# Transposing m through DRAM in every second set of a batched matrix square root

## The chip, the cores and the metric

The kernel runs on one core of a Trainium2 chip. The metric is device time in microseconds (us), and the time of a kernel is the median of its runs. Five engines work side by side, each through its own queue in order: TensorE (PE, with its weight loads shown as PEld), VectorE (DVE), ScalarE (ACT), GpSimd (POOL) and SyncE (SP), which here only issues DMAs.

## The reference

The input `x` has 32 batches of 32 channels of 128x128 matrices in f32. Two layers follow each other, each with a residual. Layer 0 normalises `x` over groups of two channels and then takes the square root of each of the 1024 matrices by five coupled Newton-Schulz steps:

```
Y = A / |A|;  Z = I
for _ in range(5):
    T = 0.5 * (3 I - Z @ Y)
    Y = Y @ T
    Z = T @ Z
x = x + Y * sqrt(|A|)
```

Layer 1 normalises again, takes a 2D Fourier transform, multiplies a few low modes by weights that mix channels, transforms back and adds to `x`. The change concerns layer 0 alone.

## The kernel before

**Tiles and sets.** A set is four channels of one batch, held as a tile of 128 partitions by 4x128 f32 (256 KB). There are 256 sets, 8 to a batch. The five Newton-Schulz steps are rewritten as matrix polynomials: a quartic in m, then an updated m, then a second quartic in the new m, and a last half step. TensorE computes `lhsT.T @ rhs`, so every product needs its left factor transposed. The kernel therefore carries m and a scaled transpose mb of it.

**One set, step by step** (`newton`, L400, and `quartic`, L364). `products` (L304) issues four 128x128 matmuls into one of eight PSUM banks; each f32 matmul is two PE instructions in the trace. `transposed` (L310) issues four PE transposes, one instruction each (L313). `taken` (L271, its operation on L276) copies a bank out on ACT with a factor. `plus` (L279, L282) copies it out on DVE with a factor and an addend. `plus_eye` (L290) makes r = mb + identity on POOL (L294 and L301).

The first quartic makes v from mb and m, needs v transposed plus r (that is w), and gives q from v and w. Then y is made from q and m, the new m from q and y. The new m is transposed on PE (`transposed(m)`), copied out as mb, and the second quartic follows with m and mb. Then come w (tile t) and y4 from q with m and y, then t from w and q, and the last product t with y is added to the input tile xt (L420).

**Far sets.** Sets of batches 1 to 18 (`is_far`, 144 sets) do not transpose v on PE. DVE transposes the 32x32 blocks of v into a tile named turn (L373), SP writes it to a DRAM tile called held (L375), SP reads it back with the blocks in their transposed places into w (one DMA on L386 for the first quartic, four DMAs of 32 partitions each on L383 for the second), and POOL adds r (L388). The first quartic reads v with a stride of four elements (`wide` is False), the second reads it in runs of 32 (`wide` is True). All other sets transpose v on PE.

**What sets the order.** The order is traced by hand: nine lanes hold one set each, the outer loop counts rounds, and in each round every lane advances its set's generator by one `yield`. `yield from rest` (rest is a pair) is two rounds. A far set has 13 such rests. A new far set may start three rounds after the last, if a lane is free. The tile framework then orders each engine's instructions by a plan of readiness, except those wrapped in `kept`, which stay in traced order: all DMA issues and the normalisation (L341, L348) among them. So SP's queue is exactly in traced order.

**Buffers.** `rooms` gives for each tile name two counts of buffers, the second from a pool that is open until 158 sets have ended (`MORE`). `four` (L263) goes round them.

**Beside it.** The same loop interleaves `prep` (statistics of the next batch), `settle` (store of xt to DRAM on L428, folds on POOL), `forward` and `spectrum` of layer 1. The later part of the kernel multiplies modes and transforms back; the change does not touch it.

Of the kernel before, what the change touches and what calls it, by code (L numbers as in the profile page):

```python
# [29 lines left out]
F32 = mybir.dt.float32  # L30
AF = mybir.ActivationFunctionType
ALU = mybir.AluOpType
# [4 lines left out]
P = 128  # L37
# [8 lines left out]
QA = 3 + 12 ** (1 / 3)  # L46
QR = 2 * QA - 9
QD = 39 / QA
EYE = 36 / 16
QS = EYE / QD  # L50
MS = -QA * QS
# [17 lines left out]
def conv_preact_kernel(  # L69
# [8 lines left out]
    nc = tc.nc  # L78

    const = ctx.enter_context(tc.tile_pool(name="const", bufs=1))  # L80
    dram = ctx.enter_context(tc.tile_pool(name="dram", bufs=1, space=DRAM))
# [5 lines left out]
    eye1 = const.tile([P, 1, P], F32, name="eye")  # L87
    nc.vector.tensor_scalar_mul(eye1[:, 0, :], ident, EYE)
    eye = eye1.to_broadcast([P, 4, P])
# [57 lines left out]
    def bank():  # L147
        return ps8.tile([P, 4, P], F32, tag="ps", name="ps")
# [36 lines left out]
    kept = tc.keep_in_program_order  # L185

    def prep(b, made):
# [12 lines left out]
        for i in range(C // 4):  # L200
# [37 lines left out]
        nc.vector.tensor_scalar_mul(  # L238
            nn, n.rearrange("p g c -> p (g c)"), P * (1.5 / EYE) ** 2
        )  # L240
# [17 lines left out]

    rooms = dict(b=(4, 2), xt=(10, 4), x=(3, 2), r=(5, 2), v=(3, 3), w=(3, 2), q=(4, 2), y=(4, 2))
    rooms.update(m=(4, 2), mb=(2, 1), t=(3, 2), y4=(2, 2), turn=(0, 4))  # L260
    turns = dict.fromkeys(rooms, 0)

    def four(tag, more):  # L263
        n, m = rooms[tag]
        if more:
            turns[tag] += 1
            if turns[tag] % (n + m) >= n:
                return early.tile([P, 4, P], F32, tag=tag + "_early", name=tag, bufs=m)
        return sets.tile([P, 4, P], F32, tag=tag, name=tag, bufs=n)

    def taken(ps, tag, more, f=1.0):  # L271
        t = four(tag, more)
        if f == 1.0:
            nc.scalar.copy(t, ps)
        else:
            nc.scalar.mul(t, ps, f)  # L276
        return t

    def plus(ps, f, t, tag, more):  # L279

        s = four(tag, more)
        nc.vector.scalar_tensor_tensor(s, ps, f, t, ALU.mult, ALU.add)  # L282
        return s

    def blocks(t):


        return t.rearrange("p c x -> p (c x)").rearrange("p (a c j) -> p a c j", a=4, c=4)

    def plus_eye(mb, far, more):  # L290

        r = four("r", more)
        if far:
            nc.gpsimd.tensor_tensor(  # L294
                blocks(r).rearrange("p a c j -> p c a j"),
                mb.rearrange("p c (a j) -> p c a j", a=4),
                eye.rearrange("p c (a j) -> p c a j", a=4),
                ALU.add,
            )
        else:  # L300
            nc.gpsimd.tensor_tensor(r, mb, eye, ALU.add)  # L301
        return r

    def products(lhsT, rhs):  # L304
        ps = bank()
        for j in range(4):
            nc.tensor.matmul(ps[:, j, :], lhsT[:, j], rhs[:, j], start=True, stop=True)  # L307
        return ps

    def transposed(t):  # L310
        ps = bank()
        for j in range(4):
            nc.tensor.transpose(ps[:, j, :], t[:, j, :], ident)  # L313
        return ps

    def is_far(b):
        return 0 < b < FIRST
# [43 lines left out]
        ready.append((xt, m, mb, plus_eye(mb, is_far(b), has_more(b, g))))  # L361
        yield

    def quartic(m, mb, r, far, more, wide):  # L364


        v = plus(products(mb, m), -1 / (QA * QR * QS), m, "v", more)
        if far:


            t = four("turn", more)
            form = "p c (b i) -> p b c i" if wide else "p c (i b) -> p b c i"
            nc.vector.transpose(blocks(t), v.rearrange(form, b=4))  # L373
            held = dram.tile([P, 512], F32, name="turn", tag="turn", bufs=8)
            kept(nc.sync.dma_start(out=held, in_=t.rearrange("p c x -> p (c x)")))  # L375
            yield from rest
            w = four("w", more)
            wb = blocks(w).rearrange("p a c j -> p a (c j)")
            if wide:
                for b in range(4):  # L380
                    rows = slice(32 * b, 32 * b + 32)
                    src = held[:, P * b : P * b + P].rearrange("(a i) x -> i a x", a=4)
                    kept(nc.sync.dma_start(out=wb[rows], in_=src))  # L383
            else:
                src = held.rearrange("(a i) (b x) -> (i b) a x", a=4, b=4)
                kept(nc.sync.dma_start(out=wb, in_=src))  # L386
            yield from rest
            nc.gpsimd.tensor_tensor(w, w, r, ALU.add)  # L388
            w = blocks(w).rearrange("p a c j -> p c a j")
        else:  # L390
            yield from rest
            w = plus(transposed(v), 1.0, r, "w", more)
        yield from rest
        q = plus(products(v, w), 1 / (16 * QS * QS), eye, "q", more)
        yield from rest
        return q

    rest = (None, None)

    def newton(g, sn, xt, m, mb, r, far, more):  # L400


        q = yield from quartic(m, mb, r, far, more, False)
        y = taken(products(q, m), "y", more, 1 / MS)
        yield from rest
        m = taken(products(q, y), "m", more, MS)
        yield from rest
        mb = taken(transposed(m), "mb", more, QR * QS / MS)
        r = plus_eye(mb, far, more)
        yield from rest  # L410
        q = yield from quartic(m, mb, r, far, more, True)
        pw, py = products(q, m), products(q, y)
        w, y = taken(pw, "t", more, 1 / MS), four("y4", more)
        for j in range(4):
            c = 4 * g + j
            nc.scalar.mul(y[:, j, :], py[:, j, :], sn[:, c : c + 1])  # L416
        yield from rest
        t = plus(products(w, q), -0.5 * EYE / 1.5, eye, "t", more)
        yield from rest
        nc.vector.tensor_tensor(xt, products(t, y), xt, ALU.add)  # L420
        yield
# [575 lines left out]
    while todo or any(lanes) or posts or specs or prods or backs:  # L997
# [3 lines left out]
        for i in range(LANES):  # L1001
            step(norms)
            step(loads)
            far = todo and is_far(todo[0][0])
            under_way = [is_far(lane[0]) for lane in lanes if lane]
            room = far or under_way.count(False) + 0.6 * under_way.count(True) < LESS
            if lanes[i] is None and todo and room and rounds >= due:
                due = max(due, rounds - 1) + (FAR if far else NEAR)
                while norms:
                    step(norms)  # L1010
                b, g = todo.pop(0)
                xt = ready[0][0]
                lanes[i] = (b, g, xt, newton(g, made[b][3], *ready.pop(0), far, has_more(b, g)))
                if stages:
                    stage()
                if not todo:
                    loads.append(weights())
            if lanes[i] is not None:
                b, g, xt, steps = lanes[i]
# [80 lines left out]
```

## Time and profile before

| what | value |
|---|---|
| median of 3 runs | 3109.61 us (3102.69 to 3109.81) |
| the profiled execution, its own time | 3100.66 us |
| span of that execution, first to last instruction | 3098.6 us |
| mean granted TensorE clock | 0.983 |
| PE busy, PEld busy | 2948.7 us, 2828.6 us |
| DVE, POOL, ACT busy | 2340.0, 1998.0, 1704.0 us |
| DMA | 636.78 MB, mean 206 GB/s |

A busy time is the union of an engine's instructions in the trace. The span can be cut into stretches of time: the far sets fill about 105 to 1610 us, the other sets and layer 1 the rest. Matmuls are pipelined, so their listed durations (about 277 ns each) overlap, and what one costs is read from the distance of starts. For SP the trace shows only issue times of DMAs; a wait of another engine for a DMA tells when it landed.

### The profile page before, as it was taken

How to read it: one execution, taken by the hardware profiler on the slowest of the kernel's cores; microseconds unless marked ns; L12 is line 12 of the kernel's file. 1: busy time of each engine (PE TensorE's matmuls, PEld its weight loads, DVE VectorE, ACT ScalarE, POOL GpSimd, SP SyncE). 2: the span in 40 equal slices, each digit the busy share in tenths (PEclk: the TensorE clock that was granted, in tenths of full speed). 3: DMA queues.
4: the chain of work that ended last, by engine and by line, in shares of the span. 5: the costliest groups of instructions: out<-in, count | busy, mean ns of one | idle time of the engine just before them, and what ended most of it. 6: DMA issues, size and time to landing. Idle time of an engine off the chain costs nothing. (4 is left out here: it accounts for less than half of the span.)

```text
span 3098.6 us, 79471 instructions
## 1 busy us (share of the span) xinstructions
PE 2948.7 (95%) x29760; PEld 2828.6 (91%) x29760; DVE 2340.0 (76%) x5178; ACT 1704.0 (55%) x4153; POOL 1998.0 (64%) x2312
## 2 busy tenths in 40 slices
PE   6999999999999999999999999999999998999994
PEld 6899999999999999999999998998899988899983
DVE  6788887888888787788877555788778766878654
ACT  3566556666665665666654444555454544555552
POOL 3567677677776666677665434768677764777453
PEclk9999999999999999999999999999999999999996
DMA  4576676666666666676743466667676876766666
GB/s 130 164 216 207 202 217 211 210 213 214 212 209 208 209 207 183 201 212 208 219 146 100 143 217 214 226 228 235 206 250 209 269 233 211 236 208 204 194 218 221
DMA packets 475150, 636.78 MB, mean 206 GB/s; under 512 B 97040, under 2 KB 255248, under 8 KB 474768
## 3 DMA queue, kind: packets, MB, share of 16 engines
q1 hardware_dynamic: 361872, 425.88, 42.8%
q10 hardware_dynamic: 112896, 205.83, 21.7%
q8 instruction: 237, 3.88, 0.5%
q14 instruction: 145, 1.19, 0.1%
HBM read 402.42 MB, written 229.11 MB: 204 GB/s over the span
## 5 line engine op out<-in xcount | busy, mean ns | idle before, releaser
L388 POOL TENSOR_TENSOR w<-w,r 128x512 f32<-128x512 f32 x288 | 366.3, 1276 | 324.3 <-DMA w<-turn 274.8
L307 PE MATMUL ps<-w,v 128*128 128x128 f32 x4096 | 554.6, 279 | 18.0 <-DVE w L282 7.7
L341 ACT ACTIVATE b<-b,a_off,a_scr 128x128 f32<-128x128 f32 x1024 | 468.7, 490 | 154.6 <-issue 48.1
L307 PE MATMUL ps<-y,q 128*128 128x128 f32 x4096 | 527.0, 277 | 6.2 <-ACT d L893 2.1
L307 PEld LDWEIGHTS ps<-w,v 128*128 128x128 f32 x4096 | 504.0, 194 | 25.1 <-POOL w L388 11.0
L307 PEld LDWEIGHTS ps<-y,q 128*128 128x128 f32 x4096 | 490.5, 193 | 9.6 <-issue 2.6
L433 POOL TENSOR_TENSOR fold<-xt 128x256 f32<-128x256 f32 x512 | 363.8, 731 | 204.5 <-DVE xt L420 192.2
L282 DVE SCALAR_TENSOR_TENSOR q<-ps,eye 128x512 f32<-128x512 f32 x512 | 348.0, 680 | 156.8 <-PE ps L307 151.5
L827 POOL TENSOR_TENSOR yt<-yt,d 128x512 f32<-128x512 f32 x248 | 311.2, 1282 | 153.7 <-ACT d L893 116.0
L301 POOL TENSOR_TENSOR r<-mb,eye 128x512 f32<-128x512 f32 x112 | 142.7, 1274 | 311.3 <-ACT mb L276 298.8
L348 POOL TENSOR_SCALAR x<-xt,a_nm,a_sc 128x128 f32<-128x128 f32 x736 | 322.7, 451 | 19.5 <-DVE a_n L231 19.5
L416 ACT ACTIVATE y<-ps,a_t_s 128x128 f32<-128x128 f32 x1024 | 291.4, 367 | 58.1 <-PE ps L307 57.6
L202 DVE BATCH_NORM_STATS2 a_st<-xs 128x6 f32<-128x128 f32 x1024 | 229.2, 278 | 108.7 <-DMA xs<-in_xt 107.9
L307 PE MATMUL ps<-m,q 128*128 128x128 f32 x2048 | 276.4, 278 | 8.1 <-DVE q L282 5.2
L307 PE MATMUL ps<-x,b 128*128 128x128 f32 x2048 | 277.0, 279 | 6.8 <-POOL x L348 5.6
L307 PE MATMUL ps<-m,mb 128*128 128x128 f32 x2048 | 276.7, 279 | 6.6 <-ACT d L893 4.3
L307 PE MATMUL ps<-x,q 128*128 128x128 f32 x2048 | 277.8, 279 | 3.3 <-DVE q L282 1.6
L307 PE MATMUL ps<-y,t 128*128 128x128 f32 x2048 | 275.1, 277 | 2.1 <-DVE t L282 2.0
L276 ACT ACTIVATE t<-ps 128x512 f32<-128x512 f32 x256 | 152.3, 595 | 223.1 <-PE ps L307 214.4
L307 PE MATMUL ps<-q,t 128*128 128x128 f32 x2048 | 274.9, 278 | 0.0
L373 DVE STREAM_TRANSPOSE turn<-v 128x512 f32<-128x512 f32 x288 | 262.0, 910 | 4.6
L307 PEld LDWEIGHTS ps<-m,q 128*128 128x128 f32 x2048 | 251.6, 193 | 10.7 <-DVE q L282 5.8
(148 smaller groups left out, 5768.2 us busy)
## 6 DMA issues: line engine op xcount, KB each, us to landing
turn<-turn SPq DMA_DIRECT2D x288, 256.0 KB
b<-in_x ACTq DMA_DIRECT2D x256, 256.0 KB
xt<-in_xt ACTq DMA_DIRECT2D x256, 256.0 KB
xs<-in_xt ACTq DMA_DIRECT2D x256, 256.0 KB
mid<-xt SPq DMA_DIRECT2D x256, 256.0 KB
yt<-mid SPq DMA_DIRECT2D x128, 512.0 KB
out<-yt SPq DMA_DIRECT2D x120, 512.0 KB
w<-turn SPq DMA_DIRECT2D x144, 256.0 KB
```

Of the source, the lines that this page charges most:

```text
L202: nc.vector.bn_stats(st[:, 4 * i + c, :], tiles[i][:, c, :])
L276: nc.scalar.mul(t, ps, f)
L282: nc.vector.scalar_tensor_tensor(s, ps, f, t, ALU.mult, ALU.add)
L301: nc.gpsimd.tensor_tensor(r, mb, eye, ALU.add)
L307: nc.tensor.matmul(ps[:, j, :], lhsT[:, j], rhs[:, j], start=True, stop=True)
L341: nc.scalar.activation(t, x, AF.Identity, bias=offset[:, c], scale=scale[:, c])
L348: nc.gpsimd.tensor_scalar(m[:, j, :], xt[:, j, :], nm[:, c // 2 : c // 2 + 1], sc[:, c : c + 1], ALU.add, ALU.mult,)
L373: nc.vector.transpose(blocks(t), v.rearrange(form, b=4))
L388: nc.gpsimd.tensor_tensor(w, w, r, ALU.add)
L416: nc.scalar.mul(y[:, j, :], py[:, j, :], sn[:, c : c + 1])
L433: nc.gpsimd.tensor_tensor(f[:, :, 64 * half : 64 * half + 64], xt[:, :, 0:64], xt[:, :, 64:128], op)
L827: engine.tensor_tensor(yh, yh, d, op)
```

## The change

`quartic` takes its two factors, the scale and the addend by argument, and its transposition through DRAM becomes a generator of its own, `turned`, which always reads v in runs of 32 and always reads back by four DMAs. `newton` uses it for the first and second quartic of all far sets. In far sets of even number (`g % TURNED == 0`, 72 of 144) `turned` also transposes m, in place of the four PE transposes. The result mt is taken as the right factor of the second quartic and its addend, so that this quartic gives the transposed polynomial, and the products behind it are in another order: w from q and mt, t from q and w, then q and t scaled (tile y4), then the last product with y. mb is taken directly from the product that gives m and serves r only. A DVE operation whose addend is mt is issued as four of 128x128, since mt lies in another layout. Such a set has 14 rests. Buffer counts change in `rooms`.

```diff
+TURNED = 2
...
+    rooms.update(mt=(0, 3), turn=(0, 4), b=(4, 1), m=(4, 2), y=(4, 4), r=(5, 3), v=(3, 4), w=(3, 2))
...
-    def quartic(m, mb, r, far, more, wide):
-        v = plus(products(mb, m), -1 / (QA * QR * QS), m, "v", more)
+    def turned(v, tag, more):
+        t = four("turn", more)
+        nc.vector.transpose(blocks(t), v.rearrange("p c (b i) -> p b c i", b=4))
+        held = dram.tile([P, 512], F32, name="turn", tag="turn", bufs=12)
+        kept(nc.sync.dma_start(out=held, in_=t.rearrange("p c x -> p (c x)")))
+        yield from rest
+        w = four(tag, more)
+        wb = blocks(w).rearrange("p a c j -> p a (c j)")
+        for b in range(4):
+            rows = slice(32 * b, 32 * b + 32)
+            src = held[:, P * b : P * b + P].rearrange("(a i) x -> i a x", a=4)
+            kept(nc.sync.dma_start(out=wb[rows], in_=src))
+        yield from rest
+        return w
+
+    def quartic(left, right, f, add, r, far, more):
+        ps = products(left, right)
+        v = four("v", more)
+        whole = len(add.shape) == 3
+        for c in [slice(0, 4)] if whole else range(4):
+            nc.vector.scalar_tensor_tensor(
+                v[:, c] if whole else v[:, c].rearrange("p (a j) -> p a j", a=4),
+                ps[:, c] if whole else ps[:, c].rearrange("p (a j) -> p a j", a=4), f, add[:, c], ALU.mult, ALU.add
+            )
         if far:
...
+            w = yield from turned(v, "w", more)
             nc.gpsimd.tensor_tensor(w, w, r, ALU.add)
...
-        m = taken(products(q, y), "m", more, MS)
-        yield from rest
-        mb = taken(transposed(m), "mb", more, QR * QS / MS)
-        r = plus_eye(mb, far, more)
...
+        pm = products(q, y)
+        m = taken(pm, "m", more, MS)
+        if far and g % TURNED == 0:
+            r = plus_eye(taken(pm, "mb", more, QR * QS), far, more)
+            mt = yield from turned(m, "mt", more)
+            mt = blocks(mt).rearrange("p a c j -> p c a j")
+            q = yield from quartic(m, mt, 1 / (QA * QA * QS), mt, r, far, more)
+            w = taken(products(q, mt), "t", more, 1 / MS)
+            yield from rest
+            t = plus(products(q, w), -0.5 * EYE / 1.5, eye, "t", more)
+            yield from rest
+            t = scaled(products(q, t), g, sn, "y4", more)
+        else:
...
         yield from rest
         nc.vector.tensor_tensor(xt, products(t, y), xt, ALU.add)
```

The `else` branch is the code of before. The DRAM tile held goes from 8 buffers to 12.

More of the change, by code (lines that the diff above doesn't have):

```diff
@@ L362, in staged @@
         yield
-    def quartic(m, mb, r, far, more, wide):
-        v = plus(products(mb, m), -1 / (QA * QR * QS), m, "v", more)
-        if far:
[L371 to L375, printed above, removed]
-            yield from rest
[L377 to L387, printed above, removed]
+    def turned(v, tag, more):
[21 more added lines that the diff above has]
+            )
+        if far:
+            w = yield from turned(v, "w", more)
             nc.gpsimd.tensor_tensor(w, w, r, ALU.add)
@@ L398, in conv_preact_kernel, with scaled @@
     rest = (None, None)
+    def scaled(ps, g, sn, tag, more):
+        y = four(tag, more)
+        for j in range(4):
+            c = 4 * g + j
+            nc.scalar.mul(y[:, j, :], ps[:, j, :], sn[:, c : c + 1])
+        return y
     def newton(g, sn, xt, m, mb, r, far, more):
-        q = yield from quartic(m, mb, r, far, more, False)
+        fm = -1 / (QA * QR * QS)
+        q = yield from quartic(mb, m, fm, m, r, far, more)
         y = taken(products(q, m), "y", more, 1 / MS)
         yield from rest
-        m = taken(products(q, y), "m", more, MS)
-        yield from rest
-        mb = taken(transposed(m), "mb", more, QR * QS / MS)
-        r = plus_eye(mb, far, more)
[L410 to L418, printed above, removed]
+        pm = products(q, y)
[11 more added lines that the diff above has]
+        else:
+            yield from rest
+            mb = taken(transposed(m), "mb", more, QR * QS / MS)
+            r = plus_eye(mb, far, more)
+            yield from rest
+            q = yield from quartic(mb, m, fm, m, r, far, more)
+            pw, py = products(q, m), products(q, y)
+            w = taken(pw, "t", more, 1 / MS)
+            y = scaled(py, g, sn, "y4", more)
+            yield from rest
+            t = plus(products(w, q), -0.5 * EYE / 1.5, eye, "t", more)
         yield from rest
```

## The prediction

> **What bounds the kernel now.** I read the page first, then the busy times of the two halves of the span, then PE's waits in the far stretch, then the timeline. Of the page, the busy shares:
>
> ```profile
> PE 2948.7 (95%) x29760; PEld 2828.6 (91%) x29760; DVE 2340.0 (76%) x5178; ACT 1704.0 (55%) x4153; POOL 1998.0 (64%) x2312
> ```
>
> The stretch in which far sets run, and the rest (columns: length; PE, PEld, DVE, ACT, POOL busy; granted clock; DMA share; GB/s):
>
> ```profile
> 105.00:1610.00 1505.00, 1484.98 (x13345) 1442.30 (x13347) 1230.00 (x2782) 909.42 (x2247) 1051.31 (x1166) 0.99 0.67 206
> 1610.00:3098.00 1488.00, 1385.12 (x15788) 1310.51 (x15788) 1041.70 (x2196) 752.61 (x1807) 902.41 (x1078) 0.97 0.65 210
> ```
>
> In the far stretch PE is busy 98.7% and its weight loads 95.8%; DVE has 18% idle, POOL 30%, ACT 40%, and the DMA engines a third. 144 sets in 1505 us are 10.45 us a set. All that PE waits for there, by the waits of PE in that window, is about 20 us:
>
> ```profile
> PE ps L307 <- POOL w L388: 7.5, 6, 3.8
> PE ps L313 <- ACT sw L472: 4.9, 4, 3.7
> PE ps L307 <- DVE xt L420: 1.9, 1, 1.9
> ```
>
> So PE's instruction rate bounds this stretch. What an instruction costs is read from starts on the timeline, not from its listed duration:
>
> ```profile
> 805.91 1.06 PE L307 MATMUL ps<-q,t 128*128 128x128 f32 x8
> 806.80 0.60 PE L313 MATMUL ps<-ident,m 128*128 128x128 f32 x4
> 807.24 1.06 PE L307 MATMUL ps<-w,v 128*128 128x128 f32 x8
> ```
>
> Eight instructions (four products) start 0.89 us apart, 0.111 us each; the four transposes of m take 807.24 - 806.80 = 0.44 us, 0.110 us each, though the page lists 277 ns for one.
>
> **What the Trainium skill says.** "Perfetto Trace Analysis", section "Identifying the Most-Contended Engine", warns that matmul busy time tells little of headroom and gives the weight-load share instead. Here both stand over 95% in the far stretch, so they agree. "TensorE: Matmul & The Clock Gate", "Part 4: PE-mode transpose", gives about 275 ns for a PE transpose in a kernel; the trace has 273 to 277 ns as duration, but 110 ns as spacing, and the spacing is the price. "VectorE: DVE Perf Modes", "The three transpose paths", says that DVE transposes only 32x32 blocks, which is why blocks have to change places through DRAM. "DMA: Bandwidth & Descriptors", "Latency and other measured facts", puts most of a DMA's fixed cost of about 2 us down to the receipt from memory, more at high load. In the far stretch the shortest time from the end of a DVE transpose to the issue of its read-back, which waits for the write to land, is 2.1 us: it agrees.
>
> **The change, part by part.**
>
> *Removed from PE.* 72 sets lose 4 transposes: 288 x 0.110 us = 31.7 us. The number of products stays at ten a set (before q m, q y, w q, t y behind the second quartic; after q mt, q w, q t, t y). A right factor in the blocked layout costs nothing new: w is one, and its products keep the 0.89 us spacing. Since PE is full, all 31.7 us lie on the path, unless PE waits more.
>
> *DVE.* A transpose has two prices on the timeline, 0.70 us in runs and 1.12 us with stride:
>
> ```profile
> 805.43 0.70 DVE L373 STREAM_TRANSPOSE turn<-v 128x512 f32<-128x512 f32 x1
> 810.05 1.12 DVE L373 STREAM_TRANSPOSE turn<-v 128x512 f32<-128x512 f32 x1
> ```
>
> All become short: 144 x 0.42 = 60 us less. New are 72 x 0.70 = 50 us. The addition of mt in four pieces has no row; 128x128 on DVE costs 0.21 us without PSUM (the eye row of the groups), a quarter of the whole operation 0.17. I bound four at 0.68 (nothing extra) to 1.12 us and take 0.90: 72 x 0.22 = 16 us. Net +6 us on 1230 of some 1475, 84% instead of 82%. It costs nothing while DVE's idle time covers it. The new transpose waits for ACT's m in the same step (0.60 us, timeline), and other sets' v, q and t stand behind it on DVE. That is under 1 us x 72, within DVE's 275 us of idle time; PE uses those results two rounds later. If that cover failed, PE would lose what the rest below prices.
>
> *ACT and POOL.* The same copies, mb now straight from the product and two rests earlier, with r on POOL; r lives longer and has eight buffers for it. Additions on L388 are as many as before. Nothing is added. Moved past: mb's copy and r now stand before the turn's DVE and SP work in the same step; both engines have room (62% and 71% of the shorter stretch).
>
> *SP.* Per set today: two writes of 0.33, one single read 0.38, four part reads 2.1 on average (1.97 to 2.88 in the timeline), the store on L428 0.56: 3.7 us of 10.45, 35%. After, per pair of sets: 5 writes 1.65, 20 part reads 10.5, 2 stores 1.1: 13.3 us of 20.5, 65%. SP is in traced order, so every read stands behind some other set's write, which waits for a DVE transpose.
>
> *DMA.* ACT's loads, 294 of 256 KB, fill 25.8% of 1000 us (DMA view, 400 to 1400 us): 0.88 us each on all engines. A turn of m adds two such, 1.76 us per 20.5: the share goes from 67% to about 77%. Bandwidth holds; latency may grow.
>
> *The rounds.* A rest more per turned set lengthens its lane by two rounds. Rounds have no time of their own; with nine sets in flight PE still has work. I cost it at nothing; without cover it would show as waits for buffers. Far sets pay no background work of layer 1's later stages, so nothing else shifts.
>
> *The new wait.* PE's product of m and mt stands four rounds behind the product that makes m, as the product of mb and m does now. Then only PE and ACT lay between; now DVE, a write, four reads. What stands behind PE's wait is everything. This is the unknown cost. What a turn takes today:
>
> ```profile
> 806.15 0.34 SPq L375 DMA_DIRECT2D turn<-turn  x1
> 811.20 0.32 SPq L375 DMA_DIRECT2D turn<-turn  x1
> 811.69 1.97 SPq L383 DMA_DIRECT2D w<-turn  x4
> 817.62 1.27 POOL L388 TENSOR_TENSOR w<-w,r 128x512 f32<-128x512 f32 x1 [0.54 <-DMA w<-turn]
> ```
>
> The turn that ended at 806.13 is written at 806.15, read only behind another set's write, at 811.69, and landed at 817.62, 11.5 us after. Today POOL's addition and one more rest (6.7 us on PE, from the transposes of m at 806.80 to m with mb at 813.50) lie behind that. For mt neither does: m was copied out by 803.49 and its next product started at 813.50, so 10.0 us are there, less about 0.9 for the DVE transpose: 9.1 us. Bounds: with the shortest parts (write landing 2.1, issue 2.0, last landing 2.0) it takes 6.1 us and PE waits for nothing; a gain below nothing is excluded, but for the 20 us that PE idles now. At today's pace it is 2.4 us late, 72 x 2.4 = 173 us. I take 0.1 us per turned set, 7 us in all, for two reasons. The 11.5 us hold over 5 us of standing in SP's queue, and which write stands ahead differs after the change. And the plan moves PE's products when it expects an operand late: ps<-q,t at 805.91 and 816.61 each follow products traced for later lanes of the round, so PE has other work to put ahead of mt.
>
> **The sum.** 3100.7 (profiled execution) - 31.7 + 7 = 3076 us. That execution is 9 us under the median of the runs, 3109.6; the forecast for the median is 3085 us, 0.8% less.
>
> **The rivals.**
> - *mt comes late (slower).* The chain above, at the product of m and mt on PE. It decides from 31.7/72 = 0.44 us a turned set on. At 1.0 us: -31.7 + 72 = +40, so 3150 us. For it: the 11.5 us against 9.1, and more DMA traffic. Against it: the plan, and the fact that PE waits for POOL's w only 7.5 us in all today. At the whole 2.4 us it would be 3251; I hold that for remote.
> - *SP or POOL takes the gain (same).* SP at 65%, in order, issues reads late, POOL waits in line for w (it does so now, 254 us from 200 to 1600 us) and PE gets w late by 0.2 to 0.4 us a far set, 29 to 58 us: about 3110 us. For it: the single read becomes four issues. Against it: PE starts two rounds after POOL's addition.
> - *The transposes were hidden or the products become slower (same).* Then PE's instructions saved would leave idle time: 3110 us. PE at 98.7% speaks against it.
> - *Everything is hidden and PE's waits shrink too:* 3109.6 - 31.7 - 8 = 3070 us.
>
> **How the numbers follow.** A measurement of this kernel can tell about 0.3%, 9 us, from no change. Forecast with its neighbours from 3065 to 3100 us: 0.66 (0.05 of it under 3070). Within 9 us: 0.14. mt late: 0.20, about half of it over 3130. The range from 3070 to 3130 us leaves out 0.05 below and some 0.10 above. Faster 0.66, same 0.14, slower 0.20.
>
> **What would show it.** PE instructions fall by 288; DVE transposes are 360, all near 0.70 us; part reads are 1440 and no single ones; the far stretch shortens by 24 us or more with PE still over 98% busy. Wrong, if PE's waits name a DMA of mt with tens of us, if PE's busy share in that stretch falls to 96% or less, or if POOL's waits for w grow together with PE's waits for POOL. If PE stays full and the stretch is no shorter, the price of a transpose was wrong.

## The result and the profile after

The changed kernel takes 3377.64 us, median of four runs (3375.84 to 3383.36), against 3108.94 us for the kernel before beside it: a ratio of 1.0872 [1.0853, 1.0892]. The forecast was 3085 us in a range of 3070 to 3130 us; the time is outside it, on the slow side. The profiled execution has a span of 3375.1 us and a mean granted TensorE clock of 0.957; before it was 3098.6 us and 0.983.

The busy shares on the page after:

```profile
PE 3022.8 (90%) x29472; PEld 2879.0 (85%) x29472; DVE 2323.6 (69%) x5466; ACT 1704.4 (51%) x4153; POOL 1996.9 (59%) x2312
```

PE has 288 instructions fewer and is busy 74 us longer. The far stretch and the rest, after (columns as in the prediction):

```profile
105.00:1849.00 1744.00, 1544.45 (x13075) 1479.62 (x13074) 1219.38 (x3070) 910.78 (x2249) 1050.51 (x1167) 0.95 0.67 200
1849.00:3375.00 1526.00, 1399.67 (x15763) 1323.12 (x15761) 1035.77 (x2193) 751.57 (x1805) 901.85 (x1077) 0.96 0.64 205
```

PE is busy 88.6% of the far stretch, where it was 98.7%. No engine has come near its limit: DVE is at 70%, POOL at 60%, and the DMA share is the same 0.67. What PE waits for in that window (us in total, times, longest):

```profile
PE ps L309 <- POOL w L397: 113.4, 71, 3.9
...
PE ps L309 <- DMA mt<-turn: 40.2, 26, 4.5
...
PE ps L309 <- POOL x L350: 23.7, 14, 3.1
```

The prediction named three signs of being wrong. Two are there: PE is busy less than 96% of the stretch, and it waits tens of us for a DMA of mt. The third is half there. PE waits for POOL's w, longer than for mt, but POOL's own waits for the reads of w did not grow; its waits for xt, ahead of its folds, did. POOL before (105 to 1610 us), then after (105 to 1849 us):

```profile
POOL w L388 <- DMA w<-turn: 274.8, 114, 8.3
POOL fold L433 <- DVE xt L420: 72.7, 52, 4.4
```

```profile
POOL w L397 <- DMA w<-turn: 254.1, 83, 7.6
POOL fold L462 <- DVE xt L449: 193.7, 64, 9.5
```

POOL works in order, so additions of w stand behind such folds. Followed back along POOL's queue to the last time that POOL stood idle, 59 of PE's 113 us come after a wait of POOL for a DMA and 55 after a wait for another engine, mostly for xt. So late reads explain about half of this wait at first hand; the rest is POOL held up by results that were late themselves.

**Where the 276 us are.** Cut both spans at the first and the last addition of w on POOL. That stretch took 1505 us before (PE busy 1485 in 13341 instructions, 111.3 ns each, idle 20) and 1741 us after (busy 1541 in 13046, 118.1 ns each, idle 200). So:

| term | us |
|---|---|
| 295 PE instructions fewer x 0.1113 | -33 |
| 13046 instructions x 6.8 ns more each | +89 |
| PE idle in the far stretch, 20 to 200 | +180 |
| after the last addition of w, 1486 to 1526 (busy +18, idle +23) | +40 |
| span | +276 |

The saving was made in full. PE then lost 180 us to idling, 2.5 us for each of the 72 turned sets, and 89 us to more time per instruction. The mean granted clock fell in the same stretch from 0.993 to 0.953. By estimate, that ratio makes 4.7 of the 6.8 ns, 61 of the 89 us (111.3 x 0.993 / 0.953 = 116.0). Some 19 us more come from counting: PE runs dry 136 times, 21 times before, and each time the last matmul counts with its listed 0.28 us instead of 0.11. The Trainium skill ("TensorE: Matmul & The Clock Gate", "Part 1: The HAM clock gate") says that the clock gate follows how busy PE has been; in these runs the kernels whose PE idles more have, on the whole, the lower clock (idle 20 us: 0.993; 137: 0.974; 200: 0.953; 214: 0.957; 517: 0.880).

**How the delay looks.** SP's queue on the timeline after (start, length of the group, number of DMAs on the right):

```profile
901.35 1.58 SPq L372 DMA_DIRECT2D turn<-turn  x2
902.99 0.42 SPq L457 DMA_DIRECT2D mid<-xt  x1
903.58 5.19 SPq L379 DMA_DIRECT2D w<-turn  x4
908.86 0.56 SPq L372 DMA_DIRECT2D turn<-turn  x1
909.47 0.43 SPq L457 DMA_DIRECT2D mid<-xt  x1
909.94 3.35 SPq L379 DMA_DIRECT2D mt<-turn  x4
913.39 2.01 SPq L372 DMA_DIRECT2D turn<-turn  x2
915.51 1.82 SPq L379 DMA_DIRECT2D w<-turn  x4
```

And on the same timeline the transpose that feeds these reads, a stall of PE, and the product that uses mt:

```profile
901.87 0.70 DVE L370 STREAM_TRANSPOSE turn<-m 128x512 f32<-128x512 f32 x1
...
908.30 1.16 PE L309 MATMUL ps<-w,v 128*128 128x128 f32 x8 [2.55 <-POOL w L397]
...
915.18 1.06 PE L309 MATMUL ps<-mt,m 128*128 128x128 f32 x8
```

The transpose of m ends at 902.57 and its read starts to be issued at 909.94, behind four reads for another set that took 5.19 us where 1.97 was shown before. The four reads of mt themselves take 3.35 us. From the transpose to PE's product are 12.6 us, where the prediction had 9.1 us to spare. This is no odd case: for the turns of m from 300 to 1500 us the mean from the end of the transpose to the landing of mt is 11.0 us.

Why do four reads take 1.8 us at one time and 5.2 us at another? SP's waits after, from 400 to 1400 us, name things that SP has no use for:

```profile
SPq L372 <- DVE turn L370: 209.9, 102, 7.0
SPq L379 <- DMA turn<-turn: 42.1, 35, 3.0
SPq L457 <- DMA b<-in_x: 20.4, 6, 7.1
SPq L379 <- DMA b<-in_x: 17.2, 13, 4.2
...
SPq L379 <- DMA xt<-in_xt: 14.7, 8, 4.2
```

b and xt are loads that ACT issues, and a read of w or mt shares no data with them. The semaphores in the trace say where the wait comes from. A completion semaphore is the counter by which a DMA tells that it has landed. The 3541 DMAs that SP and ACT issue in this execution share eight of them, dealt in turn (442 or 443 DMAs each). Of SP's 1147 DMAs from 400 to 1400 us, 1075 wait for the very semaphore that they will use, that is, until its previous DMA has landed. So a DMA is issued only when the one dealt eight places before it, of either engine, has landed. In the example the second of the four reads of w at 903.58 has the semaphore of a load of xt that ACT issued at 902.84. That load landed at 907.38, and the read was issued at 907.40.

Of SP's 71 us of waits for ACT's loads in this window, all but some 7 passed with the load already issued and under way. The DMAs themselves did not become slower: from issue to landing a load of b takes 3.8 us before and after (medians, 400 to 1400 us), a load of xt 4.7 and 4.4, a write of turn 3.3 and 3.2. But eight part reads, of 0.46 us each on average, are issued in 3.7 us, so by this estimate a queue full of them comes round to the semaphore of a load before the load has landed.

Before, the same sign stood in SP's waits, small:

```profile
SPq L383 <- DMA xt<-in_xt: 3.3, 3, 1.7
...
SPq L375 <- DMA b<-in_x: 1.4, 2, 0.8
```

### The profile page after: what moved, and what is told of

Same layout as the page of the kernel before. It is cut to its first block, busy times and chain, and to the rows that moved or that the text cites. A ratio compares the mean times of both kernels' runs of the same rounds, so it can differ in the third digit from the quotient of the medians.

```text
span 3375.1 us, 80494 instructions
## 1 busy us (share of the span) xinstructions
PE 3022.8 (90%) x29472; PEld 2879.0 (85%) x29472; DVE 2323.6 (69%) x5466; ACT 1704.4 (51%) x4153; POOL 1996.9 (59%) x2312
## 5 line engine op out<-in xcount | busy, mean ns | idle before, releaser
L309 PE MATMUL ps<-w,v 128*128 128x128 f32 x4096 | 578.0, 286 | 121.0 <-POOL w L397 113.4
L309 PE MATMUL ps<-y,q 128*128 128x128 f32 x3520 | 475.3, 281 | 2.9 <-ACT y L278 2.0
L309 PEld LDWEIGHTS ps<-y,q 128*128 128x128 f32 x3520 | 439.2, 197 | 6.9 <-issue 2.3
L309 PE MATMUL ps<-x,b 128*128 128x128 f32 x2048 | 299.7, 288 | 30.6 <-POOL x L350 29.3
L309 PEld LDWEIGHTS ps<-x,b 128*128 128x128 f32 x2048 | 270.5, 203 | 35.4 <-POOL x L350 32.1
L278 ACT ACTIVATE y<-ps 128x512 f32<-128x512 f32 x256 | 152.3, 595 | 278.2 <-PE ps L309 268.1
L278 ACT ACTIVATE m<-ps 128x512 f32<-128x512 f32 x256 | 154.0, 602 | 222.9 <-PE ps L309 210.2
L309 PEld LDWEIGHTS ps<-x,q 128*128 128x128 f32 x2048 | 260.1, 199 | 4.8 <-ACT gt L894 1.7
L391 DVE SCALAR_TENSOR_TENSOR v<-ps,x 128x512 f32<-128x512 f32 x256 | 174.8, 683 | 119.5 <-PE ps L309 111.4
L296 POOL TENSOR_TENSOR r<-b,eye 128x512 f32<-128x512 f32 x144 | 183.0, 1272 | 117.5 <-ACT b L343 105.3
```

The lines of the kernel that those rows point to most:

```text
L296: nc.gpsimd.tensor_tensor(blocks(r).rearrange("p a c j -> p c a j"), mb.rearrange("p c (a j) -> p c a j", a=4), eye.rearrange("p c (a j) - ...
L391: nc.vector.scalar_tensor_tensor(v[:, c] if whole else v[:, c].rearrange("p (a j) -> p a j", a=4), ps[:, c] if whole else ps[:, c].rearran ...
```

## The experiments

Four theories are named in the expectations. M: PE waits for mt itself, a chain too long for its distance. Q: SP's one queue has too many small DMAs to issue. R: with lanes of 30 and 28 rounds the starts fall on the same rounds and work bunches. W: the window of eight DMAs in flight. Each ratio is to the kernel before on the same chip. Diffs are against the changed kernel unless another is named. "Idle" is PE's idle time between the first and last addition of w on POOL.

This table sums SP's time from 400 to 1400 us by its issues and its waits; "loads" are ACT's b, xt and xs. "SP late" is the mean time from the end of DVE's transpose of a v to the issue of its write on SP (turns from 300 to 1500 us). The last column counts from the code the DMAs of SP and ACT together for a far set, three loads among them.

| kernel | time, us | SP issuing | waits for DVE | for other DMAs | for loads | SP late, us | DMAs a set |
|---|---|---|---|---|---|---|---|
| before | 3108.9 | 364 | 512 | 77 | 6 | 0.1 | 11 |
| after | 3377.6 | 528 | 258 | 87 | 71 | 0.9 | 16.5 |
| e1 no m turned, reads in four | 3101.6 | 492 | 340 | 95 | 19 | 0.2 | 14 |
| e18 no m turned, single reads | 3096.9 | 229 | 666 | 75 | 1 | 0.0 | 8 |
| e4 after, single reads | 3265.9 | 254 | 627 | 92 | 0 | 0.1 | 9 |
| e6 turn that nobody uses | 3383.5 | 491 | 100 | 35 | 322 | 2.5 | 16.5 |
| e9 the same, read by one DMA | 3154.8 | 540 | 249 | 112 | 47 | 0.6 | 15 |
| e10 e6 with a quarter of the bytes | 3229.5 | 548 | 133 | 38 | 231 | 1.6 | 16.5 |
| e14 e1 with five 8 KB DMAs | 3165.4 | 577 | 136 | 69 | 166 | 1.1 | 16.5 |
| e16 after, loads issued by SP | 3359.1 | 655 | 240 | 23 | 21 | 0.8 | 16.5 |

Two cautions go with all that follows. Eleven of the eighteen results lie outside every range that was set beforehand (e2, e3, e4, e5, e7, e8, e10, e11, e12, e14, e17), six between the ranges and five above them: the theories gave directions, not sizes. And the framework plans the order of POOL and DVE anew for each kernel. PE's order is the same in e6, e9 and e10 (the first 12000 instructions), but POOL's differs, by tile names, in 221 of 2312 places between e6 and e10 and in 567 between e6 and e9; between e1 and e14 it is 591. No run held it fixed, so a share of each difference may come from the plan.

### Which part of the change

**No set turns m.** All else stays: buffers, wide transposes, reads in four for both quartics.

```diff
-        if far and g % TURNED == 0:
+        if far and g % TURNED == TURNED:
```

> No far set turns m; all reads of turned tiles stay in four parts, buffers stay as after the change. Theory Q (SP's one in-order queue holds too many small DMAs, so read-backs are late): 10 turn issues per set in place of 7 before and 12.5 after, so slower than before but far better than after: 3150 to 3260 us, PE still waiting for POOL's w. Theory R (rounds: with 30 and 28 rounds a set all lanes fall on even rounds and work bunches): here every set has 28 rounds again, so about 3110. Theory M (PE waits for mt itself): mt is gone, about 3110.

Measured: 3101.62 us, 0.9985 [0.9974, 0.9997]; idle 18 us. Everything but the turn of m is free of cost, the four reads of the first quartic among it. SP issues 492 us of 1000 here and PE loses nothing, so SP's issuing is no limit at this rate.

**The first quartic's reads by one DMA,** with the strided transpose that belongs to it, as before.

```diff
+        form = "p c (b i) -> p b c i" if wide else "p c (i b) -> p b c i"
...
+            src = held.rearrange("(a i) (b x) -> (i b) a x", a=4, b=4)
+            kept(nc.sync.dma_start(out=wb, in_=src))
```

> m is turned in every second set, but the first quartic reads back by one DMA with the strided DVE transpose, as before the change: 9.5 + 4 issues a pair fewer, 27 turn issues per pair of sets in place of 33 after and 14 x 2 = 28 before... that is 13.5 in place of 16.5 a set with the store and three loads. Theory Q: most of the loss goes, 3080 to 3200 us. Theory R: the lanes still fall on even rounds, about 3330 to 3380. Theory M: mt as late as before, about 3330 to 3380.

Measured: 3295.48 us, 1.0603 [1.0569, 1.0637]; idle 137. 432 DMAs fewer give back 82 us, although these same DMAs cost nothing in e1. So what they cost depends on what stands beside them.

**A new far set after 29 rounds over nine lanes instead of 27.**

```diff
-FAR, NEAR = 27 / 9, 25 / 5
+FAR, NEAR = 29 / 9, 25 / 5
```

> Starts of far sets are spaced 29/9 rounds instead of 27/9, so that starts fall on odd and even rounds again (by the loop's rules: steps of 4, 3, 3, 3 rounds in place of 4 and 2); all DMAs stay. Theory R: most of the 268 us lost come back, 3080 to 3200 us. Theory Q: same issues, 3330 to 3400. Theory M: the same.

Measured: 3323.10 us, 1.0700 [1.0660, 1.0741]; idle 176. Wider starts take 54 us of the loss back, not the whole. Whether they are R's own is not shown: with single reads the same edit gains nothing (e7 below).

**All reads by one DMA,** mt's too (the diff of e2 with its single form for every turn).

> All three turns are read back by one DMA with the strided DVE transpose (1.12 us instead of 0.70, so DVE has about 130 us more work, some 94% of a far stretch of 1475 us). Turn issues: 5 a set in place of 12.5. Theory Q: SP has room, PE's waits for POOL's w fall to a few us; 3080 to 3180 us, with DVE as the next bound. Theory R: still on even rounds, 3330 or more. Theory M: mt no earlier, 3330 or more.

Measured: 3265.85 us, 1.0508 [1.0475, 1.0541]; idle 127. The waits for ACT's loads are gone. PE's waits from 400 to 1400 us:

```profile
PE ps L309 <- DMA mt<-turn: 42.7, 23, 4.3
PE ps L309 <- POOL x L350: 19.3, 10, 2.9
PE ps L309 <- POOL w L402: 7.2, 9, 2.5
```

Now M's wait is the first, and w hardly counts. SP is on time again (0.1 us late), yet 157 us of the loss remain. So the loss has two parts: one of 112 us that goes with the reads in four, and a larger one of some 157 us that isn't SP's lateness.

### Is it the dependency or the load

**Reads one round after the write** instead of two.

```diff
-        yield from rest
+        yield
...
+        yield
```

> All reads of turned tiles are issued one round after their write in place of two, so on odd rounds, ahead of the other sets' writes of the next even round. Number of DMAs and of rounds unchanged. If what costs is that a read stands behind another set's write in SP's queue (a form of theory R), w and mt land some 3 us earlier and most of PE's waits for POOL's w and for mt go: 3120 to 3250 us. If it is the number of issues and the waits of SP for other DMAs (theory Q), little changes: 3330 to 3390. SP may then stand longer for its own write to land.

Measured: 3435.78 us, 1.1049 [1.1023, 1.1075]. Slower, against the hope that mt comes sooner:

```profile
SPq L379 <- DMA turn<-turn: 243.0, 115, 5.0
```

SP now stands 243 of 1000 us for its own writes to land, where it stood 42, with all its later DMAs behind it.

**A turn of m that nobody uses.** m is transposed on PE in every set and each second far set also turns m into an unused tile. No wait for mt, no 30-round lane.

```diff
+            spare = turned(m, "mt", more) if far and g % TURNED == 0 else None
+            if spare:
+                next(spare)
...
+            if spare:
+                next(spare)
+                next(spare)
```

> No set uses a turned m: the second quartic takes PE's transpose as before. But every second far set still transposes m on DVE, writes it and reads it back into a tile that nobody uses, at the same places. So all the load of the change on DVE, SP and the DMA engines is there, without anyone waiting for it, and 28 rounds for every set. Theory Q (load): 3250 us or more. Theory M (the wait for mt and the longer chain of a set): about 3100 to 3140. Theory R (even rounds): about 3100 to 3140.

Measured: 3383.49 us, 1.0888 [1.0858, 1.0917]; idle 214. PE does all of its old work here, so 33 us of the difference to the changed kernel are due to that; but the load alone, without any use of mt and without R, costs as much as the whole change. M and R are not needed for a loss of this size. SP's waits from 400 to 1400 us, and PE's largest from 105 to 1750:

```profile
SPq L379 <- DMA b<-in_x: 165.4, 57, 7.4
SPq L379 <- DMA xs<-in_xt: 73.0, 44, 6.7
SPq L372 <- DVE turn L370: 65.5, 43, 6.6
```

```profile
PE ps L309 <- POOL w L397: 181.0, 97, 5.8
```

SP stands for ACT's loads longer than for DVE, in all but some 50 of the 322 us with the load already issued: that is W. SP is 2.5 us late with v's writes. PE feels it at POOL's w, but mostly in a roundabout way: POOL waits less for the reads of w than before, and in 104 of PE's 191 us (105 to 1850 us) it stands at a fold whose xt is late.

**29 rounds and single reads** (e3 and e4 together).

> Starts spaced 29/9 rounds and all reads single: the edits of e3 and e4 together. If rounds and SP's issues are two separate losses, their gains add: 3265 - 54 = about 3210 us. If both only relieve the same lateness of mt, less than that: 3230 to 3270.

Measured: 3282.80 us, 1.0549 [1.0517, 1.0581]. PE's wait for x is gone and its wait for mt has grown to 109 us (105 to 1700 us; e4 had 70). The run is 17 us slower than e4 and above both forecasts: the gains of e3 and e4 don't add.

**One set in eight turned** (18 sets).

```diff
-TURNED = 2
+TURNED = 8
```

> One far set in eight turns m (18 sets in place of 72). If each turned set costs by itself (theory M), a quarter of the 276 us against no turned set: 3101 + 69 = about 3170 us. Theory R: after a turned set lanes return to steps of 3 and the loss is under a quarter, about 3115 to 3150. Theory Q: load grows by an eighth of a turn a set and stays under what SP can take, about 3100 to 3120.

Measured: 3241.57 us, 1.0434 [1.0414, 1.0454]; idle 95. That is 133 us for 18 sets, 7.4 us each, against 3.7 us each for 72: the cost is not in proportion, and all three forecasts missed it. PE's waits (105 to 1900 us) name mt first:

```profile
PE ps L309 <- DMA mt<-turn: 44.0, 13, 8.5
```

SP is 1.1 us late here with 14.6 DMAs a set, where e1 with 14 is 0.2 us late. So the number of DMAs alone does not set the loss; when they come matters too.

### Number, bytes, distance, queue

**The spare turn with one read** instead of four: the same bytes, two DMAs instead of five (e6 with `turned(m, "mt", more, False)` and the single form of e2).

> As e6 (nobody uses the turned m), but the spare turn is read back by one DMA of 256 KB in place of four of 64 KB: 15 DMAs a set on SP and ACT in place of 16.5, the same bytes, and SP has 1.6 us less to issue per turned set. Theory W (window: a DMA of SP or ACT is issued only when the one eight places before it has landed, so the number of DMAs in a set is what counts): most of the loss of e6 goes, 3120 to 3220 us. If bytes or the load on the DMA engines count: stays at 3350 to 3390.

Measured: 3154.78 us, 1.0170 [1.0130, 1.0210]; idle 51.

**The spare turn with five DMAs and a quarter of the bytes** (against e6):

```diff
+        part = slice(0, 32) if tag == "mt" else slice(0, P)
+        kept(nc.sync.dma_start(out=held[part], in_=t.rearrange("p c x -> p (c x)")[part]))
...
+                kept(nc.sync.dma_start(out=wb[rows, 0], in_=held[part, P * b : P * b + P]))
```

> As e6, with five DMAs for each spare turn still, but a quarter of its bytes (32 rows written, 32x128 elements read by each of four DMAs). Theory W: the same number of DMAs, so still slow, 3300 to 3390 us. If bytes count: near 3120 to 3180 us.

Measured: 3229.47 us, 1.0418 [1.0378, 1.0458]. Over e1 (3101.6), five DMAs of full size cost 282 us, five of a quarter 128, two of full size 53. SP issues 491, 548 and 540 us of 1000 in the three, so the share of issuing doesn't order them; neither do bytes alone. SP's lateness does (0.2 us in e1, then 0.6, 1.6 and 2.5 for 53, 128 and 282 us). That number and time in flight both count fits a window; the changed order on POOL is not excluded.

**Single reads and one more rest** ahead of mt's use (and in the other far sets), against e4:

```diff
+            yield from rest
...
+            if far:
+                yield from rest
```

> As e4 (all reads single, m turned in every second set and used), with one more rest of two rounds between the read of mt and its use, and one more rest in the other far sets so that sets end in order. Theory M for what is left in e4 (+160 us): PE no longer waits for mt, 3110 to 3200 us. If what is left comes from the bunching of lanes on even rounds or from nine sets in flight being too few for longer sets: 3260 or more.

Measured: 3231.14 us, 1.0424 [1.0384, 1.0463]. PE's wait for mt is gone; its waits from 105 to 1700 us are now

```profile
PE ps L309 <- POOL x L350: 45.1, 22, 5.5
PE ps L309 <- POOL w L402: 26.8, 29, 4.1
```

35 us are gained of some 157. That the longer sets make the lanes start in bunches is argued, not shown.

**mt's write and single read issued by POOL** (single reads in the first quartic, four in the second; ACT's and SP's other DMAs stay):

```diff
+        queue = nc.gpsimd if tag == "mt" else nc.sync
+        kept(queue.dma_start(out=held, in_=t.rearrange("p c x -> p (c x)")))
```

> m is turned and used in every second set; its write and one single read are issued by POOL, while v's turns are read as before the change (one DMA in the first quartic, four in the second). So SP and ACT issue exactly what they did before the change. Theory W alone: the loss goes and PE's saving shows, 3075 to 3110 us. With theory M on top (mt late for PE whatever the queue): 3180 to 3260 us, PE's waits naming mt. POOL has the issue work on top of 71% busy.

Measured: 3407.42 us, 1.0998 [1.0951, 1.1044]. It leaves the eight of SP and ACT alone and is worse all the same. The first fence is PE's wait from 400 to 1400 us, the second POOL's:

```profile
PE ps L309 <- DMA mt<-turn: 68.2, 26, 6.3
```

```profile
POOL mt L385 <- DMA turn<-turn: 48.7, 23, 3.9
```

POOL's additions stand behind an issue that itself waits for mt's write to land. Both forecasts missed, and since POOL's own work suffers, this run does not speak for or against W.

### What is left, and Q against W

**Single reads, one more rest, a start every 31/9 rounds** (e11 with `FAR = 31 / 9`).

> As e11 (single reads, one more rest ahead of mt's use), with starts spaced 31/9 rounds, so 4 and 3 in place of 4 and 2. In e11 PE waited no more for mt but 45 us for x, which the next set needs two rounds after its normalisation is issued. If the bunching of starts causes that: about 3150 to 3200 us. If nine sets in flight are too few for longer sets, whatever the starts: 3220 or more.

Measured: 3185.95 us, 1.0263 [1.0243, 1.0282]; idle 71. The best version that turns m, and still 78 us slower than before. PE's waits from 105 to 1700 us:

```profile
PE ps L315 <- ACT sw L509: 40.0, 19, 4.6
```

Neither mt nor x is in front. DVE is busy 877 of 1000 us there, and SP waits 429.9 us for DVE's transposes and 137.4 us for its own writes to land.

**Five independent DMAs of 8 KB** on SP in every second far set, e1 otherwise. They use and feed nothing.

```diff
+                kept(nc.sync.dma_start(out=idle[0:16], in_=tab[0:16, 0:128]))
...
+                    kept(nc.sync.dma_start(out=few[0:16, i], in_=table[0:16, 0:128]))
```

> As e1 (no set turns m), plus five DMAs of 8 KB in every second far set on SP, one write and four reads, which wait for no engine and which nobody uses; no DVE transpose, no bytes to speak of. Theory W (number of DMAs in a window of eight): slower than e1 by half of e6's loss or more, 3200 to 3390 us. If it needs the bytes, or SP's wait for the DVE transpose of m: 3100 to 3150 us.

Measured: 3165.42 us, 1.0195 [1.0179, 1.0212]; idle 67. 64 us over e1 for 40 KB in every second set that nobody waits for. SP's waits from 400 to 1400 us:

```profile
SPq L373 <- DVE turn L371: 76.3, 59, 4.5
SPq L380 <- DMA b<-in_x: 51.6, 34, 4.2
```

Over e1, SP issues 85 us more of 1000 and stands 147 us more for loads. More of SP's added time is waiting than issuing, which speaks for W; the run does not part Q from W cleanly.

**All loads issued by SP:** the spare turn of e6, and the changed kernel.

```diff
-        kept(nc.scalar.dma_start(out=t, in_=x[b, :, 4 * g : 4 * g + 4, :]))
-        kept(nc.scalar.dma_start(out=xt, in_=xt_in[b, :, 4 * g : 4 * g + 4, :]))
+        kept(nc.sync.dma_start(out=t, in_=x[b, :, 4 * g : 4 * g + 4, :]))
+        kept(nc.sync.dma_start(out=xt, in_=xt_in[b, :, 4 * g : 4 * g + 4, :]))
```

> As e6, with the three loads per set issued by SP in place of ACT. The number of DMAs and their traced order are unchanged. Theory W in the form that any DMA waits for the one eight before to land, with latency alone the limit: 3340 or more, since SP has 1.1 us a set more to issue. In the form that SP stands because ACT issues its loads late, behind its own operations (SP waited 445 of 1400 us for loads b, xs and xt in e6): most of the loss goes, 3120 to 3250 us.

> The changed kernel itself with its three loads per set issued by SP in place of ACT. If SP standing behind ACT's late loads is a main part of the 268 us: 3180 to 3290 us, what is left being the wait for mt. If not: 3360 or more.

Measured: 3843.89 us, 1.2372 [1.2353, 1.2390], and 3359.09 us, 1.0813 [1.0794, 1.0831]. In the second, SP's waits for loads fall from 71 to 21 us of 1000 and its issuing rises from 528 to 655: nearly the same total. Which engine issues the loads matters little to the changed kernel (18 us); the first run was not followed up. Its trace has PE waiting 410 us for POOL's w (105 to 1900 us), and POOL 288 us for xt and 296 us for ACT's mb, while SP hardly waits for loads (8 us of 1000).

**Reads in four with the room of e13:** one more rest and 31/9.

> The changed kernel with the two edits that helped in e13 (one more rest ahead of mt's use and in the other far sets, starts spaced 31/9 rounds), but with its reads in four parts. If the number of DMAs is the larger cause in the changed kernel: 3290 to 3360 us, PE waiting for POOL's w. If the lateness of mt and x was: about 3190 to 3230, as in e13.

Measured: 3541.83 us, 1.1405 [1.1384, 1.1425]. More room for mt makes the changed kernel worse by 164 us, while it makes e4 better by 80. PE's waits from 105 to 1700 us:

```profile
PE ps L309 <- POOL w L397: 232.2, 116, 4.2
...
PE ps L309 <- DMA mt<-turn: 4.1, 2, 2.2
```

mt is in time and w is late, mostly behind POOL's waits for xt and mb. In SP's waits 175 of 1000 us go to loads. The four corners, in us:

| | two rests, 27/9 | three rests, 31/9 |
|---|---|---|
| mt, w read in four | 3377.6 | 3541.8 |
| single reads | 3265.9 | 3186.0 |

Single reads are worth 112 us in the left column and 356 us in the right one.

**No m turned, all reads single** (e1 and e4): the code of before with the buffers of after and eight DMAs a set on SP.

> No set turns m, and both quartics read back by one DMA with the strided DVE transpose: 8 DMAs a set in place of 11.2 before and 14.2 in e1, and DVE has 60 us more work than before. If e1 shows that 14.2 DMAs still cost nothing, fewer gain nothing either: 3095 to 3115 us. If SP's standing cost something before the change too: 3070 to 3095.

Measured: 3096.91 us, 0.9971 [0.9960, 0.9983], 9 us (0.3%) below the kernel before, about the least that such a measurement can tell. From 400 to 1400 us its PE is busy 995 of 1000 us and its granted clock is 1.00.

## Why the prediction was wrong, step by step

In short, the saving was right, and two costs were priced far too low: SP's queue was charged for its issues and not for its waits, and the way of mt from the transpose to PE was taken as nearly hidden. PE's idling then also brought the clock down, which no term had.

- **Removed from PE: right.** Instructions fell by 288, and at 0.111 us each the far stretch holds some 32 us less work. The rival "the transposes were hidden" falls.
- **DVE: right that it costs nothing.** All 360 transposes are wide, 0.65 to 0.72 us each. The addition of mt takes four pieces of 0.28 us, 1.13 us, just over the upper bound instead of the 0.90 taken. DVE's busy time fell from 2340.0 to 2323.6 us, and e1, with the wide transposes of the first quartic, lost nothing.
- **ACT and POOL: right in work, not in order.** Their busy times are the same within 2 us. But POOL stands longer for xt and for ACT's results, with w's additions behind them, and that path was in no term.
- **DMA: right.** Bandwidth held: the share stayed 0.67, not the 77% taken, because the stretch grew with the bytes. Nor did latency grow, as was feared: the median times from issue to landing are no longer than before.
- **SP: wrong, the first failed step.** The prediction put SP at 65% and priced only the issues. At 53% of issuing SP already was late. Left out of the sum was what SP stands for between issues: the DMAs of SP and ACT rose from 11 to 16.5 a set, each may go only when the one eight places before has landed, and ACT's 256 KB loads are among those eight. The rival "SP or POOL takes the gain" had this place, but the wrong size: 0.2 to 0.4 us a far set, where the reads in four alone are worth 112 us, 0.8 us a far set (e4). e6 shows that a load of this kind suffices for a loss as large as the whole.
- **The new wait: wrong, the second failed step.** 0.1 us per turned set was taken out of bounds of 0 and 2.4. Waits that name mt are 40 us in the changed kernel, 0.6 us a set, and 70 us with single reads, where SP is on time. The two reasons for the low end did not hold: the write ahead in the queue did change, yet mt lands 11.0 us after the transpose on average (9.6 with single reads) against 9.1 to spare (the 11.5 us of the forecast were one turn of v; the mean before was 9.8), and the plan could not put enough other work ahead.
- **The rounds: cause open.** "No time of their own" is in doubt: wider starts take 54 us back (e3), and with single reads POOL's x comes late (e4, e11). That this is bunching was argued from the rounds; the vanishing of the wait for x in e7 and e13 agrees, but e7 gains no time by it.
- **Time per instruction: not in the sum at all.** 89 us of the 276, some 61 of them by the lower clock, as PE idles.
- **The slower rival** had mt late at 3150 us, with 3251 as remote. It was right in kind; that its wait, the wait for w and the slower clock come together was in no case, so the time fell outside all of them.

What could be read beforehand: SP in the profile before waited in a few places for b and xt, with which it shares no data. Those were 6 us of 1000 and were passed over. They are a hint that a limit on DMAs in flight is being touched, and that added DMAs would count against it.

**What stays open.** How much of the 112 us belongs to SP's issuing and how much to the window was not parted: no run changed the number in flight. W is shown as a wait by the semaphores in the trace. As the cause of the loss it is supported by e6, e9, e10 and e14 against each other, where issuing is alike and the loss differs by five times, but POOL's planned order differs among them too, and no run held it. The larger 157 us, which remain in e4, are in part PE's wait for mt and the slower clock; what bunching adds was not parted. The Trainium skill ("DMA: Bandwidth & Descriptors", "Issuing engines are not separate DMA queues") says that issuing from several engines saves only the sequencer's time; e16 agrees with it for the changed kernel, which gains only 18 us when all loads move to SP. Why e17 loses so much more than the changed kernel, and why e15 does, is open too. The stretch after the last addition of w is 28 to 52 us longer in every kernel that uses a turned m and 5 to 16 us in those that don't (e1, e6, e9, e10, e14, e15, e18); no run looked for the cause.

With single reads and room, the turn of m still costs 78 us (e13), where the third turn in every second set fills DVE to 88%. None of the versions tried turns m at a gain.

## What to carry to other kernels

Before DMAs are added to a queue, count the DMAs per unit of work and look in that queue's waits for transfers with which it shares no data: in this case they showed a limit on transfers in flight, which the queue's share of issue time didn't. When work is moved from a full engine into a chain through DRAM, compare the chain's measured time with the measured distance of its user, and take the difference as the cost, not the hope that the order will hide it. Where a step must go through DRAM, one DMA of 256 KB was better than four of 64 KB in every pair where the queue was loaded, though it made the transpose slower (1.12 against 0.70 us).

## What the runs showed of the hardware that was not expected

- The same 512 KB, moved in every second far set in two DMAs, cost 53 us and in five 282 us over e1 (e9, e6), at 540 and 491 us of issue time in 1000; POOL's planned order differs too.
- Five DMAs of 8 KB that nothing waits for, in 72 sets, cost 64 us (e14), with the same caution.
- SP and ACT share eight completion semaphores in turn, and a DMA of one stood for a DMA of the other: 71 us of 1000 in the changed kernel, 322 in e6.
- A PE instruction, by busy time over count, in the far stretch went from 111.3 to 118.1 ns when PE's idle share there went from 1.3% to 11.5%, with the granted clock from 0.993 to 0.953.
- DMAs issued by POOL held up POOL's additions while they waited for a write to land: 84.6 us from 105 to 1700 us (e12).
